# Two graph-convolution layers on one core: nodes summed in groups of 512, and more source rows copied one by one

## The chip, the cores and the metric

The kernel runs on one core of a Trainium2 chip. The metric is the device time of one execution in microseconds (us), taken over several runs, with the median as the time. One further execution was recorded by the hardware profiler; durations of single instructions come from that one.

The engines are named as the profile names them: PE (matrix multiply; PEld is its weight load), DVE (VectorE), ACT (ScalarE), POOL (GpSimd) and SP (SyncE). Each runs its own instructions in the order in which they were put into its queue, and waits on semaphores for the others. SP and ACT can start DMA transfers from their queues (SPq and ACTq in the profile); such an issue is an instruction in the queue like any other. POOL starts the indirect transfers (gathers).

## The reference

There are 50,000 nodes with 128 features, 850,000 edges sorted by destination (50,000 of them from a node to itself), 16 relations and 8 basis matrices:

```python
def _rgcn_layer(h, src, dst, rel, basis, w_comp, loop_w, bias):
    W = jnp.einsum('rb,bio->rio', w_comp, basis)
    seg = dst.astype(jnp.int32) * N_REL + rel.astype(jnp.int32)
    agg = jax.ops.segment_sum(h[src], seg, num_segments=N_ENT * N_REL)
    agg = agg.reshape(N_ENT, N_REL, -1)
    msg = jnp.einsum('nri,rio->no', agg, W)
    out = msg + h @ loop_w + bias
    return jax.nn.relu(out)
h = _rgcn_layer(x, ...layer 1...)
h = _rgcn_layer(h, ...layer 2...)
x = _layernorm(x + h, axis=-1)
```

## The kernel before

**Chunks.** The 800,000 edges between different nodes are cut into C = 625 chunks of K = 10 tiles of 128 edges. Both layers run over all chunks, so the loop body (L925) is emitted 1,250 times. A chunk covers about 80 destination nodes. Every tile spans at most WN = 12 destination nodes, so a chunk has K*WN = 120 "slots".

**One chunk.** (a) POOL gathers the source rows of its tiles, 128 rows of 512 bytes by one indirect DMA for each tile (L202, called at L935). It is emitted FETCH = 2 chunks ahead, into one of five buffers `g`; the first gather of a chunk waits until PE has read the buffer's last content, five chunks before. (b) DVE makes `hot` (L871): for each edge, its slot and its eight basis weights. (c) PE multiplies each tile with `hot` into PSUM (L971, `pa`, two buffers, five tiles in each); ACT copies each buffer to `aT` in SBUF (L979). (d) Two chunks later PE multiplies `aT` with the eight basis matrices (L734, `ps`), and ACT copies the result to `slots` (L739). (e) DVE makes 0/1 masks `own` (L753), and PE sums slots to 128 consecutive nodes by two matmuls (L761, `pn`) that start at a register-held base of the chunk. Windows of neighbouring chunks overlap. DVE adds `ls` (L764), the part that a node gets from its own row. Layer 1 then has a Relu on ACT (L768) and a store of 128 rows to H1 (L769); layer 2 adds x (L771), normalizes with DVE and ACT (L603 to L614) and stores to the output (L775).

**A node's own part** is made by `from_itself` for 128 nodes at a time, 391 times per layer: load, a transpose on PE (L209) with a copy `hT` on ACT (L211), two matmuls of 512 columns (L710, `hb`), products with the self-edge weights on DVE (L713), a matmul with `loop_w` (L722) whose sum with the bias goes into the ninth part of `by` (L723), a reduce on DVE (L726), and a store to a DRAM tensor L (L727). Each chunk loads its 128 rows of L back by its base (L883), and in layer 2 of x too (L887).

**Rows by hand.** A chunk whose number mod 8 is 7 or 3 has only nine gathers. Its tenth tile is copied row by row by SP (mod 7) or ACT (mod 3): `row_by_row` (L789) loads 16 byte offsets into registers (L798), then issues 128 transfers of 512 bytes (L808), spread over the steps of eight chunks (L985). `by_hand` (L785) says which chunks these are.

**Order.** The order on PE, POOL, DVE and ACT is the order of the program text: inside a chunk, `beside` (L901) puts the steps of the other work between the ten matmuls of (c), and one step of each running row copy follows each matmul. So on ACT the row transfers stand between the copies of `pa`, `ps` and `hT`:

```python
for i, offset in enumerate(offsets):
    if i % step == 0:
        yield to
    behind[engine] = engine.dma_start(to.bitcast(U8)[e + i : e + i + 1, :], ...).ins
```

The transfers of SP and ACT, 45,047 in all, signal on the same eight semaphores in turn (5,630 or 5,631 on each in the trace's records), and each waits, in its queue, until the one before it on its semaphore has landed.

During layer 1, `later_rows` (L839) also prepares the edge lists of later chunks on DVE and SP, a step in each chunk.

Of the kernel before, what the change touches and what calls it, by code (L numbers as in the profile page):

```python
# [39 lines left out]
F32 = mybir.dt.float32  # L40
I32 = mybir.dt.int32
# [21 lines left out]
AHEAD = 4  # L63
# [8 lines left out]
BASES = 8  # L72
BY_HAND = 8
# [8 lines left out]
def tile_rgcn_resnorm(  # L82
# [21 lines left out]
    NG, NT = -(-R // P), -(-N // P)  # L104
# [9 lines left out]
    assert D == P and N >= P and edges.shape[0] == 1 and AT * NR == P and PER * NB * WN <= BANK and AT * PER * NB == WEIGHTS and PER == HALF and S <= P and C >= 4 and M > 0 and RUN - LK // 2 == LIVE and 2 * C <= NG * P and N <= 1 << 16 and E % ROW == 0  # L114
# [10 lines left out]
    ROW_AT = dram.tile([2 * C, P], I32, name="ROW_AT")  # L125
    NL = -(-(N + LK) // P) * P
    LREL = dram.tile([2 * NL, 1], I32, name="LREL")

    L = [dram.tile([N, D], F32, name=f"L{n}") for n in range(2)]
# [67 lines left out]
    ps_o = ctx.enter_context(tc.tile_pool(name="ps_o", bufs=1, space=PSUM))  # L197
    ps_n = ctx.enter_context(tc.tile_pool(name="ps_n", bufs=1, space=PSUM))
    ps_h = ctx.enter_context(tc.tile_pool(name="ps_h", bufs=2, space=PSUM))
# [6 lines left out]
    def turned(h, m, sb):  # L206

        tp = ps_o.tile([P, D], F32, name="po")
        nc.tensor.transpose(tp[:, :m], h, ident[:m, :m])  # L209
        hT = sb.tile([P, P], F32, name="hT")  # L210
        nc.scalar.copy(hT[:, :m], tp[:, :m])  # L211
        return hT[:, :m]
# [8 lines left out]
    key = consts.tile([P, 2 * C * HALF], BF16, name="key")  # L221


    base_i = consts.tile([1, C], I32, name="base_i")
    slot = consts.tile([P, C], F32, name="slot")
    next_slot = consts.tile([P, C], F32, name="next_slot")
    last_slot = consts.tile([P, 1], F32, name="last_slot")
    first_of = consts.tile([1, C], F32, name="first_of")
    base1 = consts.tile([1, C], F32, name="base1")
    minus = consts.tile([1, S], F32, name="minus")  # L230
# [4 lines left out]
    picked = consts.tile([P, 5 * NG + len(ROWS) + 4], F32, name="picked")  # L235
    ones = consts.tile([P, max(LIVE, C)], F32, name="ones")
# [10 lines left out]
    nc.vector.memset(minus, -1.0)  # L247
# [5 lines left out]
    def set_up(pool):  # L253
# [14 lines left out]
        po = ps_o.tile([P, D], F32, name="po")  # L268
# [146 lines left out]
    def loops_of(g, pool, m, d_i, k_f, r_i, loop, loops, asked):  # L415
# [15 lines left out]

        nc.vector.tensor_scalar(picked[0:1, 5 * g + 4 : 5 * g + 5], d_i[0:1, 0:1], float(asked()), None, op0=OP.is_ge)
        yield
# [8 lines left out]
    def rows_of(j, pool):  # L442
# [3 lines left out]
        parts = pool.tile([P, 2, LIVE, 2], F32, name="parts")  # L446
        for h in range(2):
            nc.sync.dma_start(
                parts[:m, h],
                FULL[h * NP + r0 * LIVE : h * NP + (r0 + m) * LIVE].rearrange("(p e) w -> p e w", e=LIVE),  # L450
            )
        if j:
            yield
        srcf = pool.tile([P, LIVE], F32, name="srcf")
        nc.vector.tensor_tensor(srcf[:m], parts[:m, 0, :, 0], parts[:m, 1, :, 0], op=OP.add)
        node = pool.tile([P, LIVE], I32, name="node")
        nc.vector.tensor_tensor(node[:m], parts[:m, 0, :, 1], parts[:m, 1, :, 1], op=OP.add)
# [20 lines left out]
        row_at = pool.tile([P, LIVE], F32, name="real").bitcast(I32)[:, :P]  # L478
        nc.vector.tensor_scalar(row_at[:m], srcf[:m, LIVE - P :], float(N - 1), float(4 * D), op0=OP.min, op1=OP.mult)
        nc.sync.dma_start(ROW_AT[r0 : r0 + m], row_at[:m])  # L480

# [3 lines left out]
        keyf = pool.tile([P, LIVE], F32, name="keyf")  # L485
# [6 lines left out]
        if (r0 + m) * LIVE > M:  # L492
# [6 lines left out]
                beyond[:m], place[:m, :LIVE], last[:m], 64.0, op0=OP.subtract, op1=OP.mult  # L499
# [8 lines left out]
        po = ps_o.tile([P, D], F32, name="po")  # L508
# [6 lines left out]
        nc.vector.tensor_scalar(base1[:, c0 : c0 + cs], half[0:1, :, 0], float(N - P), None, op0=OP.min)  # L515
        nc.vector.tensor_scalar(base_i[:, c0 : c0 + cs], base1[:, c0 : c0 + cs], float(4 * D), None, op0=OP.mult)

        a, b = max(c0 - 1, 0), c0 + cs - 1
        off = pool.tile([1, P], F32, name="off")
        nc.vector.tensor_tensor(off[:, : b - a], base1[:, a + 1 : b + 1], base1[:, a:b], op=OP.subtract)  # L520
        yield
        po = ps_o.tile([P, D], F32, name="po")
        for h in range(2):
            nc.tensor.matmul(po[:S, :cs], spread[h], half[:, :, h], start=h == 0, stop=False)
        nc.tensor.matmul(po[:S, :cs], minus, base1[:, c0 : c0 + cs], start=False, stop=True)
        nc.vector.tensor_scalar(slot[:S, c0 : c0 + cs], po[:S, :cs], within[:S], None, op0=OP.add)
        yield
        po = ps_o.tile([P, D], F32, name="po")
        nc.tensor.matmul(po[:, : b - a], ones[0:1, :P], off[:, : b - a], start=True, stop=True)
        nc.vector.tensor_tensor(next_slot[:S, a:b], slot[:S, a:b], po[:S, : b - a], op=OP.subtract)  # L530
        if b == C - 1:
            nc.vector.tensor_tensor(
                last_slot[:S], next_slot[:S, b - 2 : b - 1], po[:S, b - a - 1 : b - a], op=OP.subtract
            )
# [6 lines left out]
            ones[:m, :LIVE],  # L541
# [6 lines left out]
    def count_up(pool):  # L548
        last = 5 * NG + len(ROWS)
        off = pool.tile([1, C], F32, name="off_all")  # L550

        nc.vector.memset(off, float(N - 1))
        nc.vector.tensor_copy(off[:, : C - 1], first_of[:, 1:])
        nc.vector.tensor_tensor(off, off, base1, op=OP.subtract)
        nc.vector.scalar_tensor_tensor(
            off, off, float(P - 1), ones[0:1, :C], op0=OP.is_le, op1=OP.mult, accum_out=picked[0:1, last : last + 1]
        )

        in_time = pool.tile([1, C], F32, name="in_time")
        nc.gpsimd.iota(  # L560
            in_time,
            pattern=[[P * NT // C, C]],
            base=P * AHEAD - P,
# [3 lines left out]
        nc.vector.tensor_tensor(off, base1, in_time, op=OP.subtract)  # L567
        nc.vector.scalar_tensor_tensor(
            off, off, 0.0, ones[0:1, :C], op0=OP.is_le, op1=OP.mult, accum_out=picked[0:1, last + 1 : last + 2]
        )  # L570

        nc.vector.tensor_tensor(off[:, : C - 3], base1[:, 2 : C - 1], first_of[:, 1 : C - 2], op=OP.subtract)
        nc.vector.tensor_tensor(off[:, C - 3 : C - 2], base1[:, C - 1 :], first_of[:, C - 3 : C - 2], op=OP.subtract)
        nc.vector.scalar_tensor_tensor(
            off[:, : C - 2],
            off[:, : C - 2],
            1.0,
            ones[0:1, : C - 2],
            op0=OP.is_ge,
            op1=OP.mult,  # L580
            accum_out=picked[0:1, last + 3 : last + 4],
        )
        nc.vector.tensor_scalar(picked[0:1, last + 2 : last + 3], first_of[:, 0:1], 0.0, None, op0=OP.is_equal)
# [3 lines left out]
        total = ps_o.tile([P, D], F32, name="po")  # L587
# [4 lines left out]
            off[:, 1:2], total[:1, 1:2], float(E + 2 * NG * (P + 1) + 3 * C - 1), None, op0=OP.not_equal  # L592
# [3 lines left out]
    def normed(t, m, sb):  # L596

        *_, o = normed_steps(t, m, sb)
        return o

    def normed_steps(t, m, sb):
        st = sb.tile([P, 6], F32, name="st")
        nc.vector.bn_stats(st[:m], t)  # L603
        mv = sb.tile([P, 2], F32, name="mv")
        nc.vector.bn_aggr(mv[:m], st[:m])
        sd = sb.tile([P, 1], F32, name="sd")
        nc.scalar.activation(sd[:m], mv[:m, 1:2], AF.Sqrt, bias=eps[:m])  # L607
        yield
        rs = sb.tile([P, 1], F32, name="rs")
        nc.vector.reciprocal(rs[:m], sd[:m])  # L610
        nm = sb.tile([P, 1], F32, name="nm")
        nc.vector.scalar_tensor_tensor(nm[:m], mv[:m, 0:1], -1.0, rs[:m], op0=OP.mult, op1=OP.mult)
        o = sb.tile([P, D], F32, name="o")
        nc.scalar.activation(o[:m], t, AF.Identity, bias=nm[:m], scale=rs[:m])  # L614
        yield o

    def chunked():
        with (
# [8 lines left out]
            def at(c):  # L627

                if c % BASES == 0:
                    _, starts[:] = nc.values_load_multi_w_load_instructions(  # L630
                        base_i[0:1, c : min(C, c + BASES)],
                        engines=[mybir.EngineType.SP],
                        min_val=0,
                        max_val=(N - P) * 4 * D,
                        skip_runtime_bounds_check_because="bases are clamped to N - P, and no node is below 0",
                    )
                return starts[c % BASES]

            def nodes_at(of, start):
                return of.bitcast(U8).rearrange("n d -> (n d)")[ds(start, P * 4 * D)].rearrange("(p d) -> p d", p=P)  # L640

            def weights(c, n):
# [14 lines left out]
                for j in range(PER):  # L657
# [6 lines left out]
                    )  # L664
                yield pm.rearrange("e (t b) -> e t b", b=NB)

            def loop_weights(i, n):

                m = min(AT, NT - i) * NR
                rel = hp.tile([P, 2, P], I32, name="lrel")  # L670
# [544 lines left out]
```

## Time and profile before

| what | value |
|---|---|
| median of 11 runs | 20934.88 us (20917.95 to 20961.0) |
| the profiled execution | 20959.35 us, span of its instructions 20957.6 us |
| busy, share of the span | PE 54%, PEld 46%, DVE 32%, ACT 12%, POOL 55% |
| mean granted PE clock | 0.71 |
| gathers (L202) | 12,192, busy 11530 us |
| rows by hand (L808) | 19,712 on SP and 19,712 on ACT |
| DMA engines | 2 tenths busy, mean 59 GB/s |

A chunk takes 16.7 us on average in either layer (from one `aT` copy to that of the next chunk). Busy time counts what an engine computes; for SP and ACT the issue of transfers, the register loads and the waits in the queue are not in it, so an ACT that is 12% busy may still have a full queue. In a list of instructions the number after "idle before" is how long the engine stood still before that group, and the arrow names what ended most of that. In the list of waits the columns are the total, how often, and the longest, in us. "remote" stands for a release for which the profile has no instruction.

### The profile page before, as it was taken

To read this page: it belongs to the slowest core of one execution; us is meant where nothing else is said; L and a number is where in the kernel's file an instruction comes from. 1 tells how busy PE (TensorE), PEld (TensorE's weight loads), DVE (VectorE), ACT (ScalarE), POOL (GpSimd) and SP (SyncE) were. 2 spreads that over 40 slices of the span, in tenths; PEclk is the share of its full clock that TensorE was granted. 3 is DMA by queue.
4 is the path that set the end of the run, shared out by engine and by line. 5 is a ranking of instruction groups with operands and counts; after the bars stand their busy time and mean duration, and the time that the engine had idled before them with its cause. 6 is when DMAs were issued, how large, how long until landed. Compare 5 with 4: busy or idle time off the path is not lost. (4 is left out here: it accounts for less than half of the span.)

```text
span 20957.6 us, 255870 instructions
## 1 busy us (share of the span) xinstructions
PE 11420.2 (54%) x59202; PEld 9697.0 (46%) x59202; DVE 6716.8 (32%) x14585; ACT 2506.3 (12%) x6567; POOL 11556.2 (55%) x12224
## 2 busy tenths in 40 slices
PE   4555555555555555555555555555555555555555
PEld 3444444444444444444444444444444444444444
DVE  4333333333222222222233333333333333333333
ACT  0111111111111111111111111111111111111111
POOL 5555555555555555555555555555555555555555
PEclk7777676676777777767766776777777777777777
DMA  2222222222222222222222222222222222222222
GB/s 70 61 63 63 60 64 61 60 62 59 60 55 56 56 56 57 56 56 56 54 57 58 59 59 59 60 60 58 58 58 58 59 58 59 58 59 58 58 59 56
DMA packets 1236470, 1232.33 MB, mean 59 GB/s; under 512 B 318004, under 2 KB 1028332, under 8 KB 1234940
## 3 DMA queue, kind: packets, MB, share of 16 engines
q0 software_dynamic: 393696, 806.61, 15.3%
q1 hardware_dynamic: 798604, 397.62, 6.6%
q10 hardware_dynamic: 42640, 11.62, 0.2%
q8 instruction: 481, 7.88, 0.2%
q14 instruction: 1049, 8.59, 0.1%
HBM read 1059.71 MB, written 154.87 MB: 58 GB/s over the span
## 5 line engine op out<-in xcount | busy, mean ns | idle before, releaser
L971 PE MATMUL pa<-hot,g 128*128 128x96 f32 x24384 | 5453.1, 335 | 5840.0 <-issue 3085.5
L202 POOL DMA_INDIRECT g<-H,src x6096 | 5762.3, 945 | 4717.2 <-issue 1674.2
L971 PEld LDWEIGHTS pa<-hot,g 128*128 128x128 f32 x24384 | 4913.2, 255 | 7381.4 <-issue 4429.1
L202 POOL DMA_INDIRECT g<-in_x_dram,src x6096 | 5768.0, 946 | 4199.3 <-issue 1679.5
L734 PE MATMUL ps<-basis,aT 128*120 128x128 f32 x20000 | 4287.6, 353 | 85.6 <-issue 74.0
L734 PEld LDWEIGHTS ps<-basis,aT 128*120 128x120 f32 x20000 | 3671.9, 255 | 97.9 <-issue 84.1
L979 ACT COPY aT<-pa 128x480 f32<-128x480 f32 x2500 | 1395.3, 558 | 11189.8 <-DMA by_hand<-in_x_dram 4454.8
L710 PE MATMUL hb<-basis,hT 128*128 128x512 f32 x3128 | 2386.5, 856 | 43.9 <-issue 35.0
L713 DVE TENSOR_TENSOR by<-hb,lw 128x512 f32<-128x512 f32 x1564 | 1071.6, 685 | 3509.5 <-issue 1814.0
L723 DVE TENSOR_TENSOR by<-po,bias 128x128 f32<-128x128 f32 (+1 forms) x782 | 227.2, 291 | 5971.1 <-remote 3215.4
L726 DVE TENSOR_REDUCE ls<-by 128x128 f32<-128x1152 f32 (+1 forms) x782 | 1643.1, 2101 | 13.7
L871 DVE TENSOR_TENSOR hot<-fixed,own 128x960 f32<-128x960 f32 x1250 | 1446.7, 1157 | 63.9 <-issue 1.8
L209 PE MATMUL po<-ident,h_own 128*128 128x128 f32 (+1 forms) x782 | 304.7, 390 | 2125.6 <-DVE by L723 894.0
L209 PEld LDWEIGHTS po<-ident,h_own 128*128 128x128 f32 (+1 forms) x782 | 158.9, 203 | 2241.7 <-DVE by L723 982.5
L761 PE MATMUL pn<-slots,own 120*128 120x128 f32 x5000 | 967.9, 324 | 293.0 <-DVE a L764 210.2
L610 DVE RECIPROCAL rs<-sd 128x1 f32<-128x1 f32 x625 | 100.8, 161 | 2739.2 <-ACT sd L607 1743.3
L761 PEld LDWEIGHTS pn<-slots,own 120*128 120x128 f32 x5000 | 809.8, 229 | 299.8 <-DVE a L764 217.4
L710 PEld LDWEIGHTS hb<-basis,hT 128*128 128x128 f32 x3128 | 668.0, 264 | 47.7 <-issue 37.0
L658 PE MATMUL fixed<-each,is_rel 128*128 128x64 f32 x3140 | 530.4, 315 | 282.9 <-issue 278.4
L658 PEld LDWEIGHTS fixed<-each,is_rel 128*128 128x128 f32 x3140 | 501.6, 237 | 292.5 <-issue 290.5
L722 PE MATMUL po<-loop,hT 128*128 128x128 f32 x1564 | 376.5, 327 | 459.2 <-ACT hT L211 299.3
L607 ACT ACTIVATE sd<-mv,eps 128x1 f32<-128x1 f32 x625 | 184.1, 295 | 3665.6 <-DMA by_hand<-H 2566.8
(152 smaller groups left out, 4763.5 us busy)
## 6 DMA issues: line engine op xcount, KB each, us to landing
by_hand<-in_x_dram ACTq DMA_DIRECT2D x9856, 0.5 KB
by_hand<-in_x_dram SPq DMA_DIRECT2D x9856, 0.5 KB
by_hand<-H ACTq DMA_DIRECT2D x9856, 0.5 KB
by_hand<-H SPq DMA_DIRECT2D x9856, 0.5 KB
g<-in_x_dram,src POOLq DMA_INDIRECT x6096
g<-H,src POOLq DMA_INDIRECT x6096
ls_of<-L SPq DMA_DIRECT2D x1250, 64.0 KB
L<-ls SPq DMA_DIRECT2D x780, 64.0 KB
```

The costliest lines, as they stand in the source:

```text
L202: return nc.gpsimd.indirect_dma_start(out=to, out_offset=None, in_=of, in_offset=bass.IndirectOffsetOnAxis(ap=idx, axis=0))
L209: nc.tensor.transpose(tp[:, :m], h, ident[:m, :m])
L658: nc.tensor.matmul(of[:, :, j * NB : (j + 1) * NB], is_rel[:m, j * P : (j + 1) * P], EACH[n][:m], start=True, stop=True,)
L710: nc.tensor.matmul(hb[:m], hT, BASIS[n][:, b : b + few, :].rearrange("p b d -> p (b d)"), start=True, stop=True)
L713: nc.vector.tensor_tensor(by[:m, b : b + few, :], hb[:m].rearrange("p (b d) -> p b d", d=D), lw[:m, b : b + few, None].to_broadcast([m, fe ...
L722: nc.tensor.matmul(po[:m], hT, LOOP[n], start=True, stop=True)
L726: nc.vector.tensor_reduce(ls[:m], by[:m].rearrange("p b d -> p d b"), AX.X, OP.add)
L734: nc.tensor.matmul(ps[: k * WN], aT[:, b, : k * WN], BASIS[n][:, b, :], start=b == 0, stop=b == NB - 1)
L761: nc.tensor.matmul(pn, own, st[i][: ks(i) * WN], start=j == 0, stop=j == len(masks) - 1)
L871: nc.vector.tensor_tensor(hot[:, : ks(c)], pm[:, c % Q * K : c % Q * K + ks(c), :, None].to_broadcast([P, ks(c), NB, WN]), own[:, : ks(c), ...
L971: product = nc.tensor.matmul(pa[:, i * NB * WN : (i + 1) * NB * WN], g[:, k + i, :] if k + i < ks(c) - by_hand(c) else handed.pop(c), hot[ ...
L979: nc.scalar.copy(aT[:, :, k * WN : (k + m) * WN].rearrange("d b (i w) -> d i b w", w=WN), pa[:, : m * NB * WN].rearrange("d (i b w) -> d i ...
```

## The change

Nodes are now handled in 98 groups of GN = 512 (J = 4 nodes for each of 128 partitions). The ten-odd chunks that can touch a group add to one PSUM bank: masks `own` are made for each pair of a chunk and a group (1,032 per layer), and one matmul of 512 columns adds the chunk's slots to the group, for which `slots` holds four copies of a slot's sum, three of them zero. The matmul with `loop_w` goes into the same bank. A group is finished once. The tensor L, its stores and its loads are gone, `ls` stays in SBUF; the loads of x, and the stores of H1 and of the output, are of 512 nodes. `ps` has one buffer, `pn` two, `po` two (the products `hb` use them too). A chunk by SP and a chunk by ACT come every five chunks, and a register load takes 32 offsets. DVE, not ACT, copies `pa` to `aT` and turns `ps` into `slots`.

```diff
-BY_HAND = 8
+SP_EVERY = 5
+ACT_EVERY = 5
+OFFSETS = 32
...
-            HANDS = ((nc.sync, BY_HAND - 1), (nc.scalar, BY_HAND // 2 - 1))
+            HANDS = ((nc.sync, SP_EVERY, SP_EVERY - 1), (nc.scalar, ACT_EVERY, ACT_EVERY // 2 - 1))
...
+                steps = every * (K - 1)
+                for step in range(steps):
+                    for e in range(step * P // steps, (step + 1) * P // steps):
...
-                                nc.scalar.copy(
+                                nc.vector.tensor_copy(
                                     aT[:, :, k * WN : (k + m) * WN].rearrange("d b (i w) -> d i b w", w=WN),
                                     pa[:, : m * NB * WN].rearrange("d (i b w) -> d i b w", i=m, w=WN),
                                 )
...
-                st = sb.tile([P, D], F32, name="slots", bufs=5)
-                nc.scalar.copy(st[: k * WN], ps[: k * WN])
+                st = sb.tile([P, J, D], F32, name="slots")
+                nc.vector.tensor_tensor(
+                    st[: k * WN],
+                    ps[: k * WN, None, :D].to_broadcast([k * WN, J, D]),
+                    which[: k * WN, c, :, None].to_broadcast([k * WN, J, D]),
+                    op=OP.mult,
+                )
...
+            def from_itself(g, of, n):
+                m = nodes(g)
+                h = sb.tile([P, J, D], F32, name="h_own", bufs=2)
+                nc.sync.dma_start(h[:m], of_group(of, g))
...
+                for j in range(J):
+                    nc.tensor.transpose(po[:, j * P : j * P + m], h[:m, j, :], ident[:m, :m])
+                    if j % 2:
+                        yield
+                hT = sb.tile([P, J, P], F32, name="hT", bufs=2)
+                nc.scalar.copy(hT[:, :, :m], po.rearrange("p (j e) -> p j e", j=J)[:, :, :m])
...
+                        own = sb.tile([P, P], F32, name=f"own{g % 2}", bufs=2)
+                        nc.vector.tensor_scalar(
+                            own[:k], col4[:k], node4[:k, c : c + 1], float(-g * GN), op0=OP.subtract, op1=OP.is_equal
+                        )
...
+            def to_nodes(c, n):
...
+                    nc.tensor.matmul(
+                        sums[g],
+                        own,
+                        of[:k].rearrange("s j d -> s (j d)"),
+                        start=c == first(g),
+                        stop=c == final(g),
+                    )
+                    if c == first(g):
+                        hT = hTs.pop(g)
+                        for j in range(J):
+                            nc.tensor.matmul(
+                                sums[g][:m, j * D : (j + 1) * D], hT[:, j, :m], LOOP[n], start=False, stop=False
+                            )
...
+            def finish(g, n):
+                m = nodes(g)
+                ls = lss.pop(g)[:m]
+                nc.vector.tensor_tensor(ls, sums.pop(g)[:m].rearrange("p (j d) -> p j d", j=J), ls, op=OP.add)
+                if n == 0:
+                    yield
+                    nc.scalar.activation(ls, ls, AF.Relu)
+                    nc.sync.dma_start(of_group(H1, g), ls)
+                else:
+                    nc.vector.scalar_tensor_tensor(ls, ls, 0.0, xws.pop(g)[:m], op0=OP.max, op1=OP.add)
+                    yield
+                    yield from normed(ls, J, m, ls, sb)
+                    nc.sync.dma_start(of_group(out, g), ls)
...
+                def beside(t, c, owning, summing):
+                    if t in (0, 5, 7):
+                        next(owning, None)
...
+                    if t in (2, 6, 9) and ending:
+                        if next(ending[0], 0) == 0:
+                            ending.pop(0)
+                    if t == 8 and c > 2:
+                        for g in to_nodes(c - 3, n):
+                            ending.append(finish(g, n))
```

`normed` in the new form has the same operations for four nodes of a partition: statistics on DVE four times, one square root on ACT, one reciprocal and one product on DVE, and four scalings on ACT.

## The prediction

> **What bounds it now.** I read the list of waits first, since no engine is busy for more than 55% of the span.
>
> ```profile
> ACT aT L979 <- DMA by_hand<-in_x_dram: 4454.8, 718, 36.5
> ...
> PEld pa L971 <- ACT aT L979: 2899.5, 762, 17.3
> PE pa L971 <- ACT aT L979: 2725.8, 734, 17.1
> ...
> POOL g L202 <- PE pa L971: 2580.7, 412, 27.9
> ...
> ACT aT L979 <- DMA by_hand<-H: 2064.5, 756, 9.3
> ```
>
> This is a chain: ACT comes late to the copy of `pa` because row transfers stand before it in its queue, PE waits for that copy (`pa` has two buffers), and POOL waits for PE to free a gather buffer. The timeline shows one such case on ACT, PE and POOL:
>
> ```profile
> 12026.49 6.35 ACTq L808 DMA_DIRECT2D by_hand<-H  x3
> 12032.94 0.29 ACT L607 ACTIVATE sd<-mv,eps 128x1 f32<-128x1 f32 x1 [6.40 <-issue]
> 12035.69 2.01 ACTq L808 DMA_DIRECT2D by_hand<-H  x4
> 12037.80 0.56 ACT L979 COPY aT<-pa 128x480 f32<-128x480 f32 x1 [4.56 <-DMA by_hand<-H]
> ```
>
> ```profile
> 12029.09 0.58 PE L971 MATMUL pa<-hot,g 128*128 128x96 f32 x2
> 12038.41 0.74 PE L971 MATMUL pa<-hot,g 128*128 128x96 f32 x2 [8.74 <-ACT aT L979]
> ```
>
> ```profile
> 12031.34 0.94 POOL L202 DMA_INDIRECT g<-H,src  x1 [0.30 <-issue]
> 12035.02 0.94 POOL L202 DMA_INDIRECT g<-H,src  x1 [2.74 <-remote]
> 12036.27 0.94 POOL L202 DMA_INDIRECT g<-H,src  x1 [0.30 <-issue]
> ```
>
> Three rows hold ACT for 6.35 us, and PE stands still for 8.74 us until the copy. POOL needs 0.94 + 0.30 = 1.25 us per gather (12036.27 - 12035.02) when nothing holds it: 12,192 x 1.25 = 15,240 us. So 20,958 - 15,240 = 5,700 us are POOL's waits, 4.6 us of each of 1,250 chunks. No engine is a pure bound: the loop ACT, PE, DVE, SP is, through its hand-overs.
>
> What a row costs in a queue, with the eight semaphores free and not:
>
> ```profile
> 12019.41 1.21 ACTq L808 DMA_DIRECT2D by_hand<-H  x4
> ```
>
> ```profile
> 12017.09 4.79 SPq L808 DMA_DIRECT2D by_hand<-H  x14
> ...
> 12030.90 9.90 SPq L808 DMA_DIRECT2D by_hand<-H  x16
> ```
>
> An issue lasts 0.228 us (median), so four in 1.21 us are (1.21 - 0.23)/3 = 0.327 us apart; that is the pitch when free. Sixteen in 9.90 us are 0.64 apart. Over all rows that follow another row directly, the trace gives a median of 0.33 (SP) and 0.35 (ACT) and a mean of 0.62 and 0.76.
>
> **Part by part, per chunk** (1,250 of them, 16.7 us each now).
>
> *POOL.* Two fifths of the chunks, from chunk 6 on, have one gather less: 4 x 124 = 496 tiles by hand instead of 308, so 12,500 - 496 = 12,004 gathers, 9.60 per chunk. At 1.25: 12.0 us per chunk, 15,000 us in all. Around it lie 46 us before the first gather, 48 us between the layers (POOL waits for the last store of H1), 52 us after the last gather and 20 scatters of the edge lists (1.2 + 0.3 us, 30 us): 15,180 us. This is the floor. The 188 gathers saved are worth only 235 us of it; the rest must come from POOL's waits.
>
> *ACT's copies.* 2,500 copies of `pa` (558 ns) and 1,250 of `ps` (272 ns) leave ACT. That is only 1.4 us per chunk of ACT's time, but it takes three of ACT's hand-overs to PE out of each chunk. What PE still needs of ACT is `hT`, once in 512/80 = 6.4 chunks, and `lw` once in 25. DVE has no transfers in its queue.
>
> *DVE* takes 2,500 copies: bounded below by ACT's 558 ns and above by a DVE product of 512 PSUM columns (L713), 685 ns; I take 0.62 us, 1,560 us. Slots with four copies, 512 columns: 685 ns by that row, 860 us. Fewer masks (2,064 for 2,500 at 300 ns), no L723 (227 us), four times fewer and wider adds: together about -870 us. 6,717 + 1,560 + 860 - 870 = 8,270 us, 6.6 us per chunk. That lies beside POOL's 12.0.
>
> *PE.* In units of one recorded pair of 128 columns: 54.7 per chunk now (20 `pa`, 16 `ps`, 4 `pn`, 10 for the 512-column `hb`, 4.7 others). `pn` becomes 2,064 matmuls of 512 columns: 2 x 2,064 / 1,250 x 4 = 13.2 instead of 4. Sum 64.2. The stretch around 12,022 us runs a pair in 0.108 us, that around 12,041 us in 0.21: 6.9 us per chunk at the fast clock, 13.5 at the slow one. At today's mixture (mean granted clock 0.71, 9.2 us for 54.7) it is 10.8. In the trace a clock window of 3.4 us that PE fills by 95% or more is nearly always followed by a fast one, so a PE that falls behind speeds up. I hide PE behind POOL, whose five buffers let PE lag three chunks.
>
> *The row side.* This is the doubtful sum. SP and ACT each issue 248 x 128 = 31,744 rows, 25.4 per chunk instead of 15.8. At 0.327: 8.3 us. Register loads: 0.79 per chunk and engine; today's of 16 offsets take 1.16 (ACT) and 0.82 us (SP) in the mean, one of 32 lies between that and twice that. Since the two queues share semaphores, both count: 1.6 to 3.1. I take 1.8, near the row that there is. Other transfers of SP fall from 4.5 to 1.2 per chunk (the L stores and loads go, the rest is four times wider), at 0.38: 0.5. ACT's own work, 2.0 us per chunk now, becomes `hT`, Relu or root and four scalings in 6.4 chunks: 0.3. Sum 10.9 us before any wait. A wait for another engine: ACT now spends 16.7 - (15.8 x 0.327 + 1.1 + 2.0) = 8.4 us per chunk waiting, at 5.1 hand-overs, 1.65 us each. After, 2.75 hand-overs in 6.4 chunks: 0.7. Total 11.6; with double the wait 12.3.
>
> *The eight semaphores.* A row lands 1.0 us (median) after its issue ends, 1.4 at the ninth decile, so one semaphore turns over in about 1.25 to 1.7 us, and 52 transfers per chunk need 52 x 1.25/8 = 8.1 to 11 us. Beside the row side's own time, not on top.
>
> *Rarer things.* Layer 1's list preparation is unchanged, and the added stall where a group's self-edge weights must be stored first is a few times tens of us. A last group is finished by wider instructions: below 10 us.
>
> **Sum.** POOL 12.0, row side 11.6 to 12.3, PE 6.9 to 10.8, DVE 6.6. The row side and POOL are nearly equal, and where two such streams feed the same PE each waits for the other now and then; I add 0.5 us (a third of one of today's waits of 1.65): 12.5 us x 1,250 + 180 = 15,800 us. Made against the span of 20,957.6 (the execution 20,959.35, 0.1% above the median of 20,934.88), so it holds for the median too.
>
> **A rule that speaks against this.** The gathers that start while a DVE mask (L753, SBUF to SBUF) fills half of their pitch or more, 273 of them, are 1.249 us apart, and 5,732 beside a DVE that is busy for less than a fifth of it 1.249 as well. The Trainium skill, "SBUF — State Buffer", section "A bandwidth-pool intuition that's wrong", says that a DMA from GpSimd's queue that takes 620 ns alone takes 3,100 ns beside a DVE copy, because GpSimd cannot write its descriptors while DVE holds the port pair that they share. By that, DVE's 1,560 us of new copies could add that much to POOL's floor, 16,700 us. No row of this trace shows it, and the new copies read PSUM; I add nothing.
>
> **Rivals.**
>
> *The row side is the bound, still faster.* For: 52 transfers instead of 36 per chunk through eight semaphores, and every stall of one queue stops the other within eight transfers. Against: three quarters of today's other transfers go. At a mean pitch of 0.40 to 0.47: 25.4 x pitch + 3.3 = 13.5 to 15.2, so 17,000 to 19,200 us. A PE that idles just enough to stay at the slow clock lands there too: 13.5 us at 90% use is 15 us per chunk, 18,900 us.
>
> *Rows that keep today's mean pitch: slower.* The mechanism is the eight semaphores held across the queues: if ACT still stands at `hT`, Relu and the scalings with rows behind it, SP stands too. Then the pitch stays at SP's 0.62: 25.4 x 0.62 + 3.3 = 19.0 us per chunk, 24,000 us; with ACT's 0.76, 22.6 us, 28,400 us. It decides from a pitch of (16.7 - 3.3)/25.4 = 0.53 us. For: today's mean is above that. Against: that mean is made by five hand-overs per chunk, which become 0.4.
>
> *The change does not take the wait away.* PE waits for DVE's copy as it did for ACT's, since DVE itself stands at products of `hb`; then PE's extra 9.5 pairs at 9.2/54.7 = 0.17 us cost 1.6 us per chunk, and ACT's 1.4 us that leave the chain give as much back: 20,950 us. Against: DVE's waits for `hb` end with `hT`, which is made six times more rarely.
>
> **Chances.** Forecast (15,180 to 16,500) 0.53; row side or slow clock (16,500 to 19,200) 0.28; between that and today 0.07; no change 0.02; slower 0.10. The range leaves out the slower cases and the last stretch: 15,150 (30 us under the floor, for its rounding) to 19,000. A measurement tells 0.2% from no change: faster 0.88, same 0.02, slower 0.10.
>
> **What would show it.** Right: gathers 1.25 us apart over chunk borders, POOL near 72% busy (12,004 x 0.945 of 15,800), no PE wait on `aT` of 8 us, waits of ACT only at `hT`, Relu and the root; DVE near 8,300 us, its copy of `pa` at 0.56 to 0.69 us; `pn` pairs near 0.43 to 0.86 us; row pitch below 0.4. Wrong: POOL waiting for PE at most chunk borders with PE waiting for `by_hand` or `hT` (row side), or gathers themselves longer than 1.25 us (the shared port), or PE at `pa` waiting for DVE.

## The result and the profile after

| | median, us | range, us | runs |
|---|---|---|---|
| kernel before | 20931.86 | 20894.62 to 20985.76 | 31 |
| changed kernel | 24656.41 | 24649.19 to 24674.17 | 8 |

The ratio is 1.178 (95% interval 1.177 to 1.179): the change makes the kernel 17.8% slower. The forecast was 15,800 us. The profiled execution took 24,672.74 us, its span 24,671.0, mean granted PE clock 0.70.

The list of waits of the changed kernel (columns: total us, how often, longest us):

```profile
POOL g L204 <- PE pa L979: 6978.9, 438, 45.6
ACT hT L699 <- DMA by_hand<-in_x_dram: 5537.1, 80, 118.1
ACT hT L699 <- DMA by_hand<-H: 4675.5, 85, 84.3
...
PEld po L710 <- ACT hT L699: 3554.9, 143, 64.9
...
POOL g L204 <- issue: 3312.2, 10668, 32.8
...
PE pa L979 <- DVE aT L987: 2437.9, 525, 48.4
```

The chain ACT, PE, POOL is still there, only rarer and longer. ACT comes to 196 copies of `hT` instead of to 3,750 copies of `pa` and `ps`, but at each it has a queue of rows in front of it, and PE waits up to 65 us. POOL's waits for PE's `pa` are 6,979 us (2,581 before). POOL waiting for PE while PE waits for `hT` is the first of the signs that the prediction named for its being wrong.

One such wait on ACT, PE and POOL, from the timeline:

```profile
11999.96 16.07 ACTq L836 DMA_DIRECT2D by_hand<-in_x_dram  x34
12016.13 0.59 ACT L699 COPY hT<-po 128x512 f32<-128x512 f32 x1 [70.75 <-DMA by_hand<-in_x_dram]
12016.39 23.54 ACTq L836 DMA_DIRECT2D by_hand<-in_x_dram  x34
```

```profile
12016.77 2.07 PE L710 MATMUL po<-basis,hT 128*128 128x512 f32 x2 [37.03 <-ACT hT L699]
```

```profile
12023.50 0.94 POOL L204 DMA_INDIRECT g<-in_x_dram,src  x1 [32.80 <-PE pa L979]
12024.74 0.94 POOL L204 DMA_INDIRECT g<-in_x_dram,src  x1 [0.31 <-issue]
12025.99 0.94 POOL L204 DMA_INDIRECT g<-in_x_dram,src  x1 [0.30 <-issue]
```

PE stands still for 37.03 us until `hT` is there; POOL then waits 32.80 us for PE to free a buffer, and gathers at 1.25 us once it has one. The rows are what is slow: 34 rows took 16.07 us and the next 34 took 23.54 us. Each of the two groups has one register load of 2.3 us and the wait behind it inside; with these it is 0.47 and 0.70 us a row. SP's queue shows the same (33 in 15.63, 22 in 15.94).

What DVE and POOL do costs what it was expected to:

```profile
L204 POOL DMA_INDIRECT g<-H,src x6002 | 5686.4, 947 | 6474.0 <-PE pa L979 3640.6
...
L987 DVE COPY aT<-pa 128x480 f32<-128x480 f32 x2500 | 1630.0, 652 | 7775.7 <-remote 4310.9
...
L768 PE MATMUL pn<-slots,own 120*128 120x512 f32 x4128 | 2378.9, 695 | 740.7 <-DVE own L751 634.4
...
L737 DVE TENSOR_TENSOR slots<-ps,which 120x512 f32<-120x512 f32 x1250 | 856.0, 685 | 1975.8 <-remote 1571.2
```

A gather takes 947 ns, the copy 652 ns, a `slots` 685 ns, a 512-column `pn` 695 ns.

**Other chips.** The runs below were made on five chips, and there the kernel before takes 15,408 to 15,438 us (medians), not 20,930. Which chip the comparison above ran on is not on record; that it was a sixth one is inferred from its times, and it is called the chip of the comparison below. A time below is therefore compared with the time of the kernel before on the same chip, and where the 20,930 come from is a question of its own. The changed kernel itself was run on two of the five chips and is 12 and 13% slower than the kernel before there, so the sign is the same.

### The profile page after: what moved, and what is told of

Same layout as the page of the kernel before. It is cut to its first block, busy times and chain, and to the rows that moved or that the text cites. A ratio compares the mean times of both kernels' runs of the same rounds, so it can differ in the third digit from the quotient of the medians.

```text
span 24671.0 us, 282779 instructions
## 1 busy us (share of the span) xinstructions
PE 12205.2 (49%) x58712; PEld 9544.6 (39%) x58712; DVE 8247.1 (33%) x14006; ACT 421.2 (2%) x896; POOL 11402.7 (46%) x12037
## 5 line engine op out<-in xcount | busy, mean ns | idle before, releaser
L979 PE MATMUL pa<-hot,g 128*128 128x96 f32 x24008 | 4933.8, 317 | 3118.9 <-DVE aT L987 2437.9
L979 PEld LDWEIGHTS pa<-hot,g 128*128 128x128 f32 x24008 | 4580.4, 241 | 4705.2 <-DVE aT L987 2556.3
L710 PE MATMUL po<-basis,hT 128*128 128x512 f32 x3136 | 2184.3, 786 | 4719.3 <-ACT hT L699 3527.3
L987 DVE COPY aT<-pa 128x480 f32<-128x480 f32 x2500 | 1630.0, 652 | 7775.7 <-remote 4310.9
L768 PE MATMUL pn<-slots,own 120*128 120x512 f32 x4128 | 2378.9, 695 | 740.7 <-DVE own L751 634.4
L710 PEld LDWEIGHTS po<-basis,hT 128*128 128x128 f32 x3136 | 587.9, 234 | 4824.1 <-ACT hT L699 3554.9
L717 DVE TENSOR_TENSOR by<-po,lw 128x512 f32<-128x512 f32 x1568 | 1059.9, 684 | 2696.6 <-PE po L710 2414.0
L737 DVE TENSOR_TENSOR slots<-ps,which 120x512 f32<-120x512 f32 x1250 | 856.0, 685 | 1975.8 <-remote 1571.2
L670 PE MATMUL po<-each,is_l 64*128 64x32 f32 (+1 forms) x800 | 205.6, 418 | 1235.6 <-DVE is_l L661 1205.4
L751 DVE TENSOR_SCALAR own<-col,node 120x128 f32<-120x128 f32 x2064 | 541.2, 312 | 6.3 <-PE pn L768 6.3
```

Source lines behind the costliest of these rows:

```text
L710: nc.tensor.matmul(hb[:m], hT[:, j, :m], BASIS[n][:, b : b + few, :].rearrange("p b d -> p (b d)"), start=True, stop=True,)
L717: nc.vector.tensor_tensor(by[:m, b : b + few, :], hb[:m].rearrange("p (b d) -> p b d", d=D), lw[:m, j, g % T, b : b + few, None].to_broadc ...
L737: nc.vector.tensor_tensor(st[: k * WN], ps[: k * WN, None, :D].to_broadcast([k * WN, J, D]), which[: k * WN, c, :, None].to_broadcast([k * ...
L751: nc.vector.tensor_scalar(own[:k], col4[:k], node4[:k, c : c + 1], float(-g * GN), op0=OP.subtract, op1=OP.is_equal)
L768: nc.tensor.matmul(sums[g], own, of[:k].rearrange("s j d -> s (j d)"), start=c == first(g), stop=c == final(g),)
L979: product = nc.tensor.matmul(pa[:, i * NB * WN : (i + 1) * NB * WN], others.get(k + i, g[:, k + i, :]), hot[:, k + i].rearrange("e b w -> ...
```

## The experiments

The theories. **R**: the rows that SP and ACT issue set the changed kernel's time. **P**: the new work on PE and DVE does, with the clock that it gets. Later, within R: **L**, the two queues hold each other up over the shared semaphores; **C**, eight semaphores are too few; **H**, PE's wait for `hT` behind ACT's rows carries the time.

### Fewer rows, no rows, more rows, one queue

Rows in every eighth chunk:

```diff
-SP_EVERY = 5
-ACT_EVERY = 5
+SP_EVERY = 8
+ACT_EVERY = 8
```

> The changed kernel with SP and ACT each copying a tile in every eighth chunk, as before, so 19,712 rows on each queue and 12,192 gathers. Theory R (the row queues set the time: 31,744 rows of 0.64 us in the mean, 1.9 ms of register loads and 2 ms of other things fill SP's 24.7 ms): SP needs 19,712 x 0.64 + 616 x 1.87 + 2,000 us = 15,800 us, POOL 12,192 x 1.25 + 180 = 15,420 us, so 15,800 to 17,500 us. Theory P (the 512-column sums on PE and the copies and products on DVE set it, rows are incidental): 24,000 us or more.

No rows (`by_hand` returns an empty list; every tile is gathered by POOL):

```diff
-                if ks(c) < K:
+                if True:
                     return []
```

> The changed kernel with no tile copied by rows, 12,500 gathers. Theory R: POOL's 12,500 x 1.25 + 180 = 15,800 us is the floor, and 15,800 to 16,800 us the time, POOL back to back over chunk borders. Theory P: about 24,000 us, with PE waiting for DVE as now.

The kernel before with rows as often as in the changed one (its 128 rows spread over 45 steps):

```diff
-BY_HAND = 8
+BY_HAND = 5
+OFFSETS = 16
...
```

> The kernel before with only the row copies of the change: a tile by SP and one by ACT in every fifth chunk, spread over 45 steps, 16 offsets per register load; sums, copies on ACT and the tensor L stay. Theory R: SP needs 31,744 x 0.64 + 1,984 x 0.85 + 5,600 other transfers at 0.5 = 24,800 us, and ACT has its copies in the queue as well: 24,800 to 29,000 us. Theory P: the saved 188 gathers and little else, 20,700 to 21,000 us.

The changed kernel with SP's rows only:

```diff
-                return [i for i, (_, every, at) in enumerate(HANDS) if c > every and c % every == at]
+                return [i for i, (_, every, at) in enumerate(HANDS) if i == 0 and c > every and c % every == at]
```

> The changed kernel with SP's row copies alone (31,744 rows on SP, none on ACT), 12,252 gathers. If rows are slow because gathers stretch each issue, SP's mean pitch stays at 0.6 us or above and the time at 23,000 to 24,700 us. If they are slow because the two queues hold each other up through the eight semaphores, the pitch falls to 0.33 to 0.45 us and the time to 16,300 to 18,200 us. Theory P: 24,000 us.

Measured, beside 15,437.96 us for the kernel before:

| run | us | ratio (95% interval) |
|---|---|---|
| rows every 8 | 15446.68 | 1.0005 (0.9996 to 1.0015) |
| no rows | 15829.43 | 1.0254 (1.0236 to 1.0271) |
| before, rows every 5 | 19069.66 | 1.2354 (1.2329 to 1.2378) |
| rows on SP alone | 15522.76 | 1.0056 (1.0036 to 1.0076) |

Theory P falls on this chip: without rows, or with 19,712 of 31,744 on each queue, all the new work of PE and DVE fits beside POOL, whose pace is 12,500 x 1.25 + 180 = 15,805 us with no rows. The kernel before becomes slow by the rows alone, and more so than the changed kernel, which takes 17,310 and 17,450 us on two other chips of the five (below): at the same number of rows the rest of the change is worth 1,600 to 1,800 us (loads of 32 offsets for 16 are in that). Two of the four expectations under theory R had reckoned with a pitch of 0.64 us and came out too high: 15,800 us or more for rows every 8, and 24,800 or more for the kernel before with more rows. SP alone was faster than the 16,300 us expected at least, though its pitch of 0.33 us was as expected.

### The kernels as they are, and with POOL or the rows taken out

> The changed kernel itself, beside the kernel before on the same chip. On a chip where the kernel before takes about 15,440 us, as in the first four experiments, theory R (the row queues set the time, and their price is the chip's: steps of 0.71 us in the issue of rows on the one, none on the other) expects 31,744 x 0.40 + 992 x 2.16 + 2,000 us = 16,800 us on SP, so 15,300 to 17,800 us; on a chip where the kernel before takes 20,900 us, 24,600 us. Theory P (sums and copies on PE and DVE) was left without support by the first four and expects 24,000 us on either.

> The kernel before itself, for its profile on this chip. Theory R: where it takes 15,440 us, rows of both queues have no pitches near 0.72, 1.43 and 2.13 us, their mean is 0.35 to 0.55 us, and POOL runs back to back over chunk borders (12,192 x 1.25 + 180 = 15,420 us). Where it takes 20,900 us, the steps are there and the means are 0.6 to 0.8 us.

The changed kernel with one gather per chunk in place of nine or ten. It leaves most edges out of the sums; the other tiles hold zeros:

```diff
-                        for k in range(ks(to) - len(by_hand(to))):
+                        for k in range(1):
...
```

> The changed kernel with one gather per chunk; the other tiles of a chunk are read from buffers that were set to zero once, so the sums leave most edges out. What is left is the row side beside PE, DVE and ACT. If rows are slow because running gathers stretch each issue, their pitch falls to 0.33 to 0.47 us and the time to 13,500 to 15,500 us; if the two row queues stretch each other, nothing changes against the changed kernel on the same chip.

The kernel before without rows:

> The kernel before with no tile copied by rows, 12,500 gathers, ACT's queue free of transfers. Theory R: POOL's floor of 12,500 x 1.25 + 180 = 15,800 us on any chip, up to 16,300; so on a chip where the kernel before takes 20,900 us all of the 5,100 us between are the rows' price, and where it takes 15,440 us the rows save 2.4%. If other hand-overs of PE, DVE and ACT bind the kernel before, 18,000 us or more.

Measured, beside 15,411.08 us for the kernel before: changed 17,308.39 (ratio 1.123, 1.121 to 1.125); before again 15,437.38; few gathers 16,399.41; before without rows 15,784.28 (one execution each of the last three).

The kernel before on this chip, from its list of waits:

```profile
POOL g L202 <- issue: 3555.1, 11647, 0.3
ACT aT L979 <- DMA by_hand<-in_x_dram: 3150.8, 725, 28.7
...
ACT aT L979 <- DMA by_hand<-H: 1926.8, 903, 6.8
```

POOL works back to back: its only waits of weight are 0.3 us of issue, 11,647 times, and 12,192 x 1.25 + 180 = 15,420 us is its time. ACT still waits over 5,000 us behind rows, but POOL does not wait for that. So on this chip there was nothing to regain but the saved gathers.

The changed kernel with few gathers:

```profile
POOL g L204 <- PE pa L981: 13975.3, 1172, 49.5
```

With POOL at rest for 14 of 16.4 ms the time is still 1,220 us above POOL's pace of the full kernel (15,180). PE, DVE and ACT do their full work here, but without rows this work fits into 15,800 us; what takes 16,400 is the rows: theory R. Restoring the gathers adds 910 us. The time lies between the two expected ones, and SP's mean pitch is 0.375 us for 0.398 in the full kernel: gathers stretch the rows a little, and most of the excess stays without them.

### No rows and the change again, ACT alone, every sixth chunk

> The changed kernel with no tile copied row by row, all gathers on POOL. If the rows set the time of the change wherever it runs (theory R), this is POOL's own pace, 12,500 gathers x 1.25 + 180 = 15,800 us, whatever the kernel before takes on the same chip, 15,420 or 20,930. If the masks on DVE, PE and the clock carry a part (theory P), it is above 17,500 us wherever the kernel before takes 20,930. Where the kernel before takes 20,930 and this 15,800, the rows are the whole of the difference between the two times of the kernel before as well.

> The changed kernel as it is. Theory R ties its time to the mean pitch of the rows: about 17,300 us at 0.40 us a row, about 24,650 where a part of the rows takes a step of 0.7 us more and the mean is 0.6 or above. A theory that puts the time elsewhere has no reason for the time to follow the pitch.

ACT alone is the edit of SP alone with `i == 1`; every sixth chunk sets both constants to 6.

> Only ACT copies a tile row by row, in every fifth chunk; SP copies none. If two queues hold each other over the eight semaphores, one queue alone keeps 0.33 us a row, as SP alone did, and the kernel ends near POOL's pace, 12,248 x 1.25 + 180 = 15,490 us, perhaps 15,600 with what ACT's instructions wait behind its rows. If ACT's queue is slow in itself, its mean pitch stays at 0.40 or above, and PE goes on waiting for hT; 16,000 us or more.

> Both queues copy in every sixth chunk. Rows and loads of a queue are five sixths of the changed kernel's: 26,450 rows x 0.40 + 826 loads x 2.2 + 1,700 = 14,100 us by theory R, below POOL's pace of 12,083 x 1.25 + 180 = 15,285 us, so POOL sets the time, 15,300 to 15,400 us, 0.3 to 0.9% below the kernel before where that takes 15,420. With a mean pitch of 0.64 the same sum is 20,400 us, close to the 20,930 of the kernel before there. By theory P the time would stay near the changed kernel's.

Measured, beside 15,410.25 us for the kernel before:

| run | us | ratio (95% interval) |
|---|---|---|
| no rows | 15802.37 | 1.0254 (1.0237 to 1.0272) |
| changed | 17451.01 | 1.1324 (1.1301 to 1.1346) |
| rows on ACT alone | 18159.19 | 1.1783 (1.1759 to 1.1807) |
| rows every 6 | 15306.62 | 0.9933 (0.9917 to 0.9950) |

Rows in every sixth chunk are **faster than both kernels** here, by 0.7% against the kernel before (0.5 to 0.8%: a small gain, but clear of the noise). Its list of waits shows POOL with 11,706 waits of issue out of 12,088 gathers, and PE no longer long at `hT`:

```profile
POOL g L204 <- issue: 3591.1, 11706, 19.3
...
PEld po L710 <- ACT hT L699: 442.3, 71, 26.3
```

So 206 tiles on each queue fit and 248 do not: the step from POOL's pace (15,290) to 17,300 lies between one sixth and one fifth.

ACT alone was expected to behave as SP alone and is slower than both queues together. The median pitch is 0.326 us, so its queue is not slow in itself, but 469 gaps of more than 3 us hold 4,310 us. The records tell which transfer had used a waiting row's semaphore last: for 734 waits (4,490 us over the pitch) it was a load of SP's (`rel`, `h_own`, `xw`, `lrel`) that itself had stood in SP's queue waiting for its buffer and had been issued a median of 2.3 us before. That is mechanism L, shown with one row queue. C is not at work here, since the same eight semaphores let SP alone issue its rows at a mean pitch of 0.333 us. A row of ACT waits for an unrelated transfer of SP because the eight semaphores are dealt out in turn over both queues. SP alone has no such waits, since ACT issues no other transfers. ACT is late at `hT` by it, and PE behind ACT:

```profile
PEld po L710 <- ACT hT L699: 5557.9, 195, 56.8
...
ACT hT L699 <- DMA by_hand<-in_x_dram: 4127.1, 93, 81.6
```

### The order of the rows, and hT on DVE

Pairs: the rows of both queues are emitted one by one, in equal numbers in each step; turns of nine: the same with eight or nine rows of SP, then of ACT, in every third step.

```diff
-                                for each in fetching.values():
-                                    next(each, None)
+                                for _ in range(rows_due(c, k + i)):
+                                    for each in fetching.values():
+                                        next(each, None)
...
```

> The rows of the two queues are put in the program's order one by one, SP's, ACT's, SP's, instead of two or three at a time, so that the round of eight semaphores gives each queue four of its own almost all the time; number of rows, loads and gathers as in the changed kernel. If the queues hold each other over shared semaphores (theory L), the waits on the other queue's rows go, the mean pitch falls from 0.40 towards 0.33 to 0.35, and a queue needs 31,744 x 0.34 + 992 x 2.2 + 1,700 = 14,700 us, below POOL's pace of 15,180: 15,250 to 15,800 us. If eight semaphores are simply too few (theory C), nothing but the order changes and the pitch stays at 0.39 or above: 16,400 to 17,400 us. If PE's wait for hT carries it (theory H), 17,300 us.

> The opposite order: eight or nine rows of SP, then as many of ACT, so that each row waits for a row that the other queue issued. Theory L: each queue passes the other's turn in full, mean pitch about 0.6 us, 31,744 x 0.6 + 2,200 + 1,700 = 23,000 us, bounds 19,000 and 25,000. Theories C and H: within 2% of the changed kernel's 17,310 to 17,450 us.

```diff
-                nc.scalar.copy(hT[:, :, :m], po.rearrange("p (j e) -> p j e", j=J)[:, :, :m])
+                nc.vector.tensor_copy(hT[:, :, :m], po.rearrange("p (j e) -> p j e", j=J)[:, :, :m])
```

> The changed kernel with the 196 copies of hT on DVE instead of ACT, so that PE no longer waits for an instruction that stands behind ACT's rows; 196 x 0.7 = 0.14 ms more on DVE. Theory H: PE's 3,100 us of waits for hT go, and the time falls by 1,000 to 2,100 us, to 15,200 to 16,300. Theories L and C: the rows set the time, and it stays within 1.5% of 17,310 to 17,450 us.

> Both edits together. Where pairs alone leave a wait for hT behind ACT's rows, this takes it away: theory L gives POOL's pace, 15,180 to 15,400 us, 0.1 to 1.5% below the kernel before where that takes 15,420. Theory C: as pairs alone, 16,400 us or more.

Measured, beside 15,408.42 us for the kernel before: pairs 17,401.41 (ratio 1.130, 1.128 to 1.131); turns of nine 17,437.89 (1.132, 1.130 to 1.134); `hT` on DVE 17,460.25 (1.133, 1.131 to 1.135); pairs and `hT` on DVE 17,436.91 (1.132, 1.130 to 1.133).

The two orders tell nothing apart, because the edit did not reach what it was meant to change: of the rows whose semaphore had last served a row, it was one of the same queue in 74.3% of cases in the changed kernel, 74.4% with pairs and 74.6% with turns of nine. The text's order is not the order in which the semaphores are dealt out between queues. L against C in the two-queue kernel stays undecided by these two.

`hT` on DVE does tell: theory H falls. From the list of waits of the changed kernel (the run of 17,451 us), and from that with `hT` on DVE:

```profile
PEld po L710 <- ACT hT L699: 3114.4, 189, 42.5
```

```profile
ACT sd L587 <- DMA by_hand<-H: 5061.0, 80, 90.0
ACT ls L792 <- DMA by_hand<-in_x_dram: 4774.3, 81, 100.7
...
PEld po L710 <- DVE hT L699: 892.2, 102, 43.8
```

PE's wait for `hT` falls from 3,114 us (the run of 17,451) to 892, and the time does not move (ratio 1.133; 1.123 and 1.132 for the changed kernel). ACT's queue stays full of rows and its next instructions (`sd`, Relu) are late. PE's long wait, the most visible thing in the profile after, was a symptom. The reading that fits is that the tiles copied by rows come late anyway.

### Longer and shorter stops

```diff
-OFFSETS = 32
+OFFSETS = 16
```

> The changed kernel with register loads of 16 offsets in place of 32: 1,984 loads a queue at about 1.27 us (the price in the kernel before) in place of 992 at 2.17, so 0.37 ms more in each queue. If each queue pays only its own stops, 17,350 + 370 = 17,700 us. If each stop is paid by the other queue too over the shared semaphores (theory L), 17,350 + 740 = 18,100 us or more.

> Loads of 8 offsets: 3,968 a queue at an estimated 0.82 us (by the same line through 2.17 us for 32 and 1.27 for 16), 3.25 ms in place of 2.15, 1.1 ms more in each queue. Each queue paying its own: 18,450 us. Theory L: 19,500 us or more, and the time over 0.327 us a row at rows whose semaphore the other queue used last grows, where C and the own-stops reading leave it alone.

Measured, beside 15,408.76 us for the kernel before: 16 offsets 17,053.96 (ratio 1.107, 1.104 to 1.110); 8 offsets 17,284.80 (1.122, 1.118 to 1.125).

Both expectations were wrong: loads of 16 make it faster, by 250 and 400 us against the two times of the changed kernel (17,308 and 17,451, on other chips), and loads of 8 leave it about where it was, though each queue now spends more time in loads. Where SP's queue spends its time, worked out from the records (in ms; a row counts up to 0.327 us, what is over that stands apart; the parts of a column add up to the span by the way they are made; 17,449 is the span of the profiled execution of the run of 17,451):

| SP's queue | changed, 17,449 | 16 offsets | 8 offsets | SP alone | changed, 24,671 |
|---|---|---|---|---|---|
| 31,744 rows at up to 0.327 us | 10.30 | 10.31 | 10.31 | 10.25 | 10.03 |
| register loads | 2.20 | 2.60 | 3.36 | 2.23 | 1.98 |
| over that, first row after a load | 1.34 | 0.53 | 0.54 | 0.09 | 1.33 |
| over that, row after a row | 2.34 | 2.34 | 1.87 | 0.31 | 9.79 |
| other transfers, waits, rest | 1.27 | 1.26 | 1.19 | 2.65 | 1.54 |
| sum = span | 17.45 | 17.05 | 17.27 | 15.52 | 24.67 |

The first row after a load shows L at work in the two-queue kernel: of its 1.34 ms, 1.33 lie at the 924 rows (of 992) whose semaphore a row of the other queue had used last. It comes 1.68 us after a load of 32 on the mean, 0.60 after one of 16, 0.46 after one of 8, and 0.41 after one of 32 when SP is alone. While a queue loads for 2.16 us the other issues 2.16/0.327 = 6.6 rows; the eight semaphores have then nearly gone round, and the first row finds its own in use. The expectation had every stop paid a second time in proportion to its length; in fact only a long stop is, and by the queue that made it, when it comes back. So the excess of SP's rows whose semaphore a row of the other queue had used last, which was expected to grow, falls from 2.3 ms to 1.1 with loads of 8. At 16, the loads cost 0.40 ms more and this wait 0.81 ms less, and the rest is the same to 0.01 ms: 0.41 ms gained. Against the changed kernel's other profile (17,303 us: 1.30 and 2.25 ms over the pitch) it is 0.26 ms. Both queues' waits of a row after a row (2.34 and 2.45 ms) have either queue's earlier row on the semaphore, for SP 1.21 ms its own and 0.98 ms one of ACT; whether they are L or C was not separated.

## Why the prediction was wrong

**The floor of POOL held.** 1.25 us per gather and 180 us around them give 15,805 us for the 12,500 gathers without rows (15,802 and 15,829 measured), and 15,290 for the 12,088 of every sixth chunk (15,307 measured). Saved gathers are worth what was said. The changed kernel never reaches the floor.

**DVE held**: 8,247 us busy for 8,270 worked out, the copy 652 ns for 0.62 us, `slots` 685 ns.

**PE held**: it could hide behind POOL. Without rows PE does the same 58,712 matmuls within 15,802 us, busy for 79% of the span, and POOL waits for its `pa` 22 us in all:

```profile
PE pa L979 <- DVE aT L987: 85.7, 194, 2.4
...
POOL g L204 <- PE pa L979: 21.9, 72, 0.3
```

The granted clock is 0.85 there; with the rows it is 0.78 in the run of 17,449 us, where PE is busy for 60%, and 0.70 at 24,671 us, where it is busy for 49%. So the low clock goes with a PE that stands still more; that it sets the time no run shows. (In the prediction 54.7 - 4 + 13.2 is 63.9, not 64.2, which changes none of its times by more than 0.1 us per chunk.)

**The rule on the shared port did not apply.** No-rows runs with all of DVE's new copies end at POOL's pace, with gathers of 946 to 949 ns:

```profile
L204 POOL DMA_INDIRECT g<-in_x_dram,src x6250 | 5932.2, 949 | 1934.7 <-issue 1837.0
L204 POOL DMA_INDIRECT g<-H,src x6250 | 5913.3, 946 | 1923.5 <-issue 1852.5
```

The up to 1,560 us that the Trainium skill, "SBUF — State Buffer", section "A bandwidth-pool intuition that's wrong", would have added by the prediction's estimate do not appear; adding nothing was right. The new copies read PSUM; what a copy between two SBUF tiles would do to the gathers no run here shows.

**The row side's sum is the step that failed, in its term for waits.** Per chunk, against SP's queue in the run of 17,449 us: rows 8.3 and 8.24 measured; loads 1.8 and 1.76; other transfers and own work 0.5 + 0.3 and 1.0 (waits of these transfers in it). These held. Waits were put at 0.7, doubled 1.4, and measured (2.34 + 1.34)/1.25 = 2.95 us. So 11.6 became 13.96 us, above POOL's 12.0 instead of beside it, and 1,250 x 13.96 = 17,450. This sum is the span by the way it is made; that the rows' side sets the time is shown by the runs without rows and with few gathers. The 0.7 counted waits of ACT for other engines. What it left out is the row queues' waits for semaphores, which "the eight semaphores" had put "beside the row side's own time, not on top". They are on top. On the chip of the comparison the same term is (9.79 + 1.33)/1.25 = 8.9 us where the prediction had 0.7 to 1.4, and the sum 19.7; most of the 8.9 are the steps of the last section.

**"That mean is made by five hand-overs per chunk" is refuted for SP, and for ACT explains a part at most.** This argument set aside the rival that gave 24,000 us at a pitch of 0.62. With the hand-overs gone from ACT, the mean pitch on the same chip is 0.638 us on SP (0.619 before) and 0.576 on ACT (0.761 before). And where it takes 15,437 us the kernel before, with all its hand-overs, has 0.391 on SP and 0.490 on ACT. The rival had the price: 25.4 x 0.638 + 3.3 = 19.5 us per chunk, 24,400 us, for 24,656 measured. That it came so near was in part luck, since its mechanism was half of it: the queues do hold each other over the semaphores, but ACT's standing at `hT` does not decide the time where that was tried, and most of the excess here is of another kind (last section).

**The rival "the change does not take the wait away"** named DVE as the engine that PE would wait for. PE's waits for `aT` (2,438 us) do remain, but without rows, on another chip, they are 86 us: they follow from the rows.

**Where the gain was read from.** The 5,700 us of POOL's waits were read as the price of ACT's copies, and so as a gain to be had. Where the rows are faster, the kernel before runs at POOL's pace with all of these copies on ACT (15,437 us). So they were the price of slow rows, which the change asks for 1.6 times as often (31,744 for 19,712 on each queue). The mean pitch of 0.62 was in the prediction; the bounds should have used it until a row showed what makes it go.

## What to carry to other kernels

A queue of small transfers costs its issue pitch times their number, plus what it waits for shared semaphores: use the measured mean pitch, not the median of the undisturbed ones, until the cause of the difference is shown to go. Transfers of two queues that draw semaphores from one round stop each other, also by transfers that have nothing to do with each other; so look up which queue used a waiting transfer's semaphore last, and keep stops in such queues short. Work moved off a gather engine pays only while the queue that takes it stays below the gather engine's pace: here one chunk in six did, one in five did not.

## What the runs showed that was not expected

**The same kernel, 15,410 or 20,930 us.** On the chip of the comparison a part of the rows' instructions take a step of about 0.70 us, on top of or in place of their usual time. Below are the register moves that precede the rows, and the rows, of SP in layer 1; the three numbers are min/median/max in ns. First the changed kernel there:

```profile
L836 SPq MOVE by_hand<-in_x_dram x15872: 1/29/1466, 55.2 to 12479.1; - x199
L836 SPq DMA_DIRECT2D by_hand<-in_x_dram x15872: 1/228/1777, 55.3 to 12479.1; - x199
```

and the same kernel at 17,449 us:

```profile
L836 SPq MOVE by_hand<-in_x_dram x15872: 29/29/42, 55.2 to 8788.7; - x199
L836 SPq DMA_DIRECT2D by_hand<-in_x_dram x15872: 224/228/2654, 55.3 to 8788.7; - x199
```

A move waits for no semaphore. Of SP's 31,744 moves 3,476 take more than 0.5 us there (median of these 0.70 us), in the kernel before 2,487 of 19,712; none does in any profile of the experiments. The excess of a row after a row is 9.79 ms there for 2.34 here, and this difference of 7.4 ms is that of the two spans (24,671 - 17,449 = 7.2 ms). Moves, issues of rows and gaps ahead of a move that last over 0.5 us, none of them a wait for a semaphore, come to 2.5, 2.7 and 2.4 ms among these rows of SP, and to 0.01 ms at 17,449 us. So the steps carry the difference between the two places. What they are was not found: they are not waits for a semaphore, since the moves have them too; the packets of 512 bytes are not slow, 25 to 27 ns (median) in both places, though the time to landing can't be compared, since the trace of the chip of the comparison holds 87,546 landings on the eight semaphores and the other 139,309; and they are more frequent while POOL gathers (SP's mean pitch 0.82 us, 0.47 without). No experiment ran where the kernel before takes 20,930 us, so what takes the steps away, and whether every sixth chunk would win there, is open.

**A register load costs a fixed part and a part per offset**: 2.16 us for 32, 1.26 for 16, 0.80 for 8, about 0.34 + 0.057 per offset. The cheapest per offset was not the fastest: 16 beat 32 and 8.
